# Three edits to a two-layer graph network kernel: score order in the last attention block, the last projections of layer 0, and the size of the written parts of q and k

## The chip, the cores and the metric

The kernel runs on one core of one Trainium2 chip. The metric is the device time in microseconds of one execution. PE is the matrix engine, DVE the vector engine, ACT the scalar engine, POOL the GpSimd engine and SP the sync engine, which here issues nearly all DMAs.

## The reference, cut to what matters

`x` is 3327 x 128, `adj` is a 3327 x 3327 matrix of zeros and ones. Each layer is followed by a residual and a norm.

```
# layer 0: attention by cosine over the neighbours
cos = beta * (x @ x.T) / (norm(x) @ norm(x).T + 1e-7)
x = layernorm(x + softmax(cos + (1 - adj) * -1e9) @ x)
# layer 1: attention among nodes, for d = 128 "heads" of h = 8 features
q = (x @ Wq.T).reshape(d, n, h); k = ...; v = ...
a = softmax(einsum('dnh,dmh->dnm', q, k) * d ** -0.5 + adj + adj)
out = einsum('dnm,dmh->dnh', a, v).reshape(n, h * d)
x = layernorm(x + out @ Wo.T)
```

Layer 1 has 128 score matrices of 3327 x 3327. Each needs the maximum of its rows, the exponential, and the product with v, so it is nearly the whole of the time.

## The kernel before

**Layer 0** goes over 26 tiles (T) of 128 nodes. Its loop `for t in range(-2, T + 3)` is a software pipeline: in one iteration, tile t has its scores made, tile t - 1 its weights turned and summed (`turn_weights`, `weigh0`), tile t - 2 its norm (`norm_begin`, `norm_root`, `norm_end`) and the turn of its result x1 (`project_turn`), and tile t - 3 its projection to q, k and v in six pieces of 512 columns (`project`, lines 344 to 361). All projection pieces and the turn use one PSUM bank, `pq`: a piece is a matmul, then a copy on ACT into `row`, and after two pieces a DMA of `row` to q_s, k_s or v_s in DRAM. Inside an iteration, k counts eight slots. The last two iterations of the loop hold nothing but the tail of tiles 24 and 25.

**Parting q and k** (`prepare`, lines 812 to 846) reads q_s and k_s back by heads, 16 pieces (`works`) in all. POOL reorders one into `by_t`, PE turns it 128 columns at a time, four to a chunk (`turn`), and ACT and DVE part each chunk of 512 columns in `high` (rounded to float32r) and `low` (the rest). Both are written to qp_s or kp_s, one DMA of SP each, 2 KB to a row; seven chunks make a piece, the last with 256 columns. `high` and `low` have four buffers each. Between pieces the first maxima of layer 1 are searched, and the first units are loaded.

**Layer 1** goes over 9 blocks of up to 3 tiles of queries; the last block has 2 tiles (256 queries). A block has 32 units of 4 heads each. A unit has 26 steps, one for each tile of keys. All engines take their instructions in the order in which the code writes them. A step of unit u does this:

- `shifts`: writes the negative row maxima, in three bf16 parts, in PSUM by matmuls with 3 rows; in `eb` (two heads, hs_b), later in `ea` (the two others, hs_a). Line 700.
- `scores`: adds the products of keys and queries (float32r, 32 rows a head). Line 706.
- `search`: products for the maxima of a later unit, 33 steps ahead, each reduced by DVE: a pair, `max_pair`, of two heads in the PSUM tile m2 (reduction line 619), and a single, `max_single`, in m1 (line 640). Both show as `m` on line 604. m1 and m2 have one buffer each.
- `pb`: exponential of eb on ACT (line 917), multiplied on POOL with the exponential of the adjacency (line 918).
- `add_adj`: adds twice the adjacency to ea on PE (line 687); then its exponential `pa`, one of each head (line 946).
- `weigh`: products of the step before the last with v, in `acc` (line 717).

`eb` has one buffer of two heads, `ea` one buffer for each of its two heads. When the maxima are searched for blocks of three tiles (`full`), each step has a pair and a single; the pair goes behind eb's shifts and the single behind ea's. For the last block, the single goes behind eb's shifts in each step and the pair behind ea's in every second one; this is the case for the last 33 steps of block 7 and all of block 8 but its last 33 steps, which have nothing to search. The heads of pair and single are chosen so that they use other rows of the array than the work beside them.

Of the kernel before, what the change touches and what calls it, by code (L numbers as in the profile page):

```python
# [19 lines left out]
P = 128  # L20
# [26 lines left out]
def gnn_two_layers(  # L47
# [118 lines left out]
    with ExitStack() as l0:  # L166
# [174 lines left out]
        def project_turn(t: int):  # L341
            u = tiles[t]
            tp = ps_x.tile([P, 512], F32, name="pq")
            nc.tensor.transpose(tp[:, :P], u.x1, ident)
            u.x1T = ptp.tile([P, P], F32, name="x1T")
            nc.scalar.copy(u.x1T, tp[:, :P])
# [16 lines left out]
        with tc.manual_schedule(  # L363
            engines={
                mybir.EngineType.PE,
                mybir.EngineType.Activation,
                mybir.EngineType.DVE,
                mybir.EngineType.Pool,
            }
        ):  # L370
            xn = big.tile([P, T, D], F32, name="xn")
            nc.gpsimd.memset(xn[:, T - 1, :], 0.0)
            w = (T - 1) * P
            nc.sync.dma_start(xn[:, : T - 1, :], x[:w].rearrange("(t p) d -> p t d", p=P))
            nc.sync.dma_start(xn[: N - w, T - 1, :], x[w:])
            xs = work.tile([P, T, D], F32, name="s")
            nc.gpsimd.memset(xs[:, T - 1, :], 0.0)
            xf = xs.rearrange("p t d -> p (t d)")
            for part, width in node_parts():
                nc.sync.dma_start(xf[part, :width], node_blocks(x, part, width))  # L380
            nbeta = const.tile([P, 1], F32, name="nbeta")
            nc.sync.dma_start(
                nbeta, bass.AP(tensor=beta.tensor, offset=beta.offset, ap=[[0, P], [1, 1]])
            )
            ones = const.tile([P, P], F32, name="ones")
            nc.gpsimd.memset(ones, 1.0)
            minus = const.tile([P, 1], F32, name="minus")
            nc.gpsimd.memset(minus, -1.0e9)
            for t in range(3):
                load(t)  # L390
            for t in range(2):
                load_bits(t)
            ws = []
            for name, wT in (("wq", wqT), ("wk", wkT), ("wv", wvT)):
                wt = big.tile([P, C], F32, name=name)
                nc.sync.dma_start(wt, wT)
                ws.append(wt)


            nc.gpsimd.tensor_mul(xs, xs, xs)  # L400
            norm_q = const.tile([P, T], F32, name="norm_q")
            nc.vector.reduce_sum(norm_q, xs, axis=AX.X)
            nc.scalar.activation(norm_q, norm_q, AF.Sqrt)

            nc.vector.tensor_scalar_max(norm_q, norm_q, 1e-20)
            by_q = const.tile([P, T], F32, name="by_q")
            nc.vector.reciprocal(by_q, norm_q)
            norm_c = const.tile([P, T], F32, name="norm_c")
            nc.vector.tensor_scalar_mul(norm_c, by_q, 1e-7)
            nc.vector.tensor_scalar(by_q, by_q, nbeta, -1.0, op0=ALU.mult, op1=ALU.mult)  # L410
            xT = big.tile([P, NP], F32, name="xT")
            sqT = work.tile([P, NP], F32, name="s")
            for c in range(NCH):
                tp, a, b = turn(ps_tp, lambda t: xn[:, t, :], c)
                cols = slice(a * P, b * P)
                tp = tp.rearrange("p t k -> p (t k)")
                copy(c, xT[:, cols], tp)
                nc.gpsimd.tensor_mul(sqT[:, cols], xT[:, cols], xT[:, cols])
            norm_k = big.tile([P, NP], F32, name="norm_k")
            for j in range(NPC):  # L420
                nc.scalar.activation(piece(norm_k, j), score_piece(ones, sqT, j), AF.Sqrt)
            nc.scalar.preload_act_table_set("natural_log_exp_and_others")

            for t in range(-2, T + 3):

                def there(n: int):
                    return 0 <= n < T

                for k in range(8):
                    if k == 0:  # L430
                        if there(t - 1):
                            weights(t - 1, 0)
                        if there(t - 3):
                            project(t - 3, 0)
                        if there(t - 2):
                            norm_begin(t - 2)
                        if there(t):
                            scores(t, 0)
                        if there(t - 1):
                            turn_weights(t - 1, 0)  # L440
                            weights(t - 1, 1)
                        if there(t - 3):
                            project(t - 3, 1)
                        if there(t - 2):
                            norm_root(t - 2)
                        continue
                    if there(t) and k < NPC:
                        scores(t, k)
                    if there(t - 1):
                        if k < NCH:  # L450
                            turn_weights(t - 1, k)
                        weigh0(t - 1, k - 1)
                    if k == 1 and there(t - 2):
                        norm_end(t - 2)
                    if there(t + 1):
                        for step, *i in {
                            1: ((inverse_log,),),
                            2: ((inverse_exp, 0),),
                            3: ((inverse_exp, 1), (inverse_product, 0)),
                            4: ((mask,), (inverse_newton, 0)),  # L460
                            5: ((inverse_product, 1),),
                            6: ((inverse_newton, 1),),
                        }.get(k, ()):
                            step(t + 1, *i)
                    if k < 5 and there(t - 3):
                        project(t - 3, k + 1)
                    if k == 5 and there(t - 2):
                        project_turn(t - 2)
                    if there(t + 2):
                        for i in {4: (0,), 5: (1, 2), 6: (3, 4), 7: (5, 6)}.get(k, ()):  # L470
                            adj_chunk(t + 2, i)
                    if k == 5 and there(t + 3) and t >= 0:
                        load(t + 3)
                if there(t + 4) and t + 4 > 1:
                    load_bits(t + 4)
# [8 lines left out]
    with ExitStack() as at:  # L484
# [166 lines left out]
        def search(step):  # L651
            if step is not None:
                (max_pair if len(step[1]) == 2 else max_single)(*step)
# [120 lines left out]
        with tc.manual_schedule(  # L774
# [27 lines left out]
            with ExitStack() as pr:  # L802
# [12 lines left out]
                def prepare(i):  # L815
# [9 lines left out]
                    for c in range(NCH):  # L825
                        tp, a, b = turn(ps_tp, lambda t: by_t[:, t], c)
                        tp = tp.rearrange("p t k -> p (t k)")
                        cols = slice(a * P, b * P)
                        n = (b - a) * P
                        high = work.tile([P, 512], F32R, name="high", bufs=4)[:, :n]  # L830
                        low = work.tile([P, 512], F32R, name="low", bufs=4)[:, :n]
                        nc.scalar.copy(high, tp)
                        nc.vector.tensor_sub(low, tp, high.bitcast(F32))
                        for i, part in enumerate((high, low)):
                            if b == T:

                                nc.vector.tensor_copy(
                                    part[:, n - 1 : n], part[:, n - 1 - P : n - P].bitcast(F32)
                                )
                            nc.sync.dma_start(  # L840
                                dst[g * HG : (g + 1) * HG, :, i, cols].rearrange(
                                    "d f n -> (d f) n"
                                ),
                                part.bitcast(F32),
                            )

                k = 0
                load_heads(0)
# [45 lines left out]
            for s in range(NU * T + LAG):  # L894
                i, j = divmod(s, T)
                u = us.get(i)
                if u is not None:
# [13 lines left out]
                    e_b = ps_b.tile([P, 2, 512], F32, name="eb")  # L911
                    b01 = [e_b[:, x] for x in range(2)]
                    shifts(u, b01, hs_b)
                    search(first)
                    scores(u, j, b01, hs_b, True)
                    pt_b = pp.tile([P, 2, QB], F32, name="pb")
                    nc.scalar.activation(pt_b[:, :, : u.nq], e_b[:, :, : u.nq], AF.Exp)  # L917
                    nc.gpsimd.tensor_tensor(  # L918
# [4 lines left out]
                    )  # L923
                    e_a = new_a()
                    shifts(u, e_a, hs_a)
                    search(late)
                    scores(u, j, e_a, hs_a, False)
                    free = e_a[0][:, QB:]
                    x = us.get(i + 1)
# [123 lines left out]
```

## Time and profile before

| | us |
|---|---|
| median of 3 runs | 15599.28 |
| lowest, highest | 15595.41, 15599.93 |
| the profiled execution | 15613.45 |
| its span, first to last instruction | 15611.6 |

| stage of the profiled execution | from, to (us) |
|---|---|
| layer 0 | 0 to 715 |
| parting q and k | 727 to 989 |
| layer 1, blocks of 3 tiles | 989 to 14225 |
| layer 1, last block | 14225 to 15505 |
| output projection | 15505 to 15612 |

Busy over the span: PE 98%, DVE 89%, POOL 89%, ACT 81%. Ends of matmuls are modelled, so a full PE row does not tell that the matrix array is full. In the views, x behind a group is a count of instructions, and "idle before <-releaser" names what ended an engine's wait.

### The profile page before, as it was taken

Reading aid. Unit: us, or ns where it says so; the run is one execution under the profiler, and the core shown is the slowest. Engines: PE = TensorE matmul, PEld = TensorE weight load, DVE = VectorE, ACT = ScalarE, POOL = GpSimd, SP = SyncE. Lnnn points to the kernel's source line nnn. Section 1 sums busy time; section 2 is a strip of 40 time slices with the busy share of each in tenths; the row PEclk is TensorE's granted clock in tenths of the full one; section 3 lists DMA queues with packets and bytes.
Section 4 is the critical chain, followed back from the end, with each engine's and each line's share of the span. In section 5 each row is a group of like instructions: output and inputs, shape, how many; then the busy total and the mean of one; then the engine's idle time right before and its main releaser. Section 6 shows DMA issues by size and latency. Waiting matters only on the chain.

```text
span 15611.6 us, 508271 instructions
## 1 busy us (share of the span) xinstructions
PE 15342.4 (98%) x217532; PEld 6892.6 (44%) x217532; DVE 13898.5 (89%) x16311; ACT 12601.3 (81%) x24955; POOL 13899.2 (89%) x9625
## 2 busy tenths in 40 slices
PE   8879999999999999999999999999999999999999
PEld 6634444444444444444444444444444444444555
DVE  7679999999999999999999999999999999998776
ACT  7658888888888888888888888888888888888776
POOL 0059999999999999999999999999999999999886
PEclk9879999999999999999999999999999999999999
DMA  7651111111111111111111111111111111111112
GB/s 207 204 199 47 48 51 53 50 46 50 52 51 46 50 49 54 50 46 50 53 50 46 50 53 49 50 46 56 46 50 46 50 53 50 48 48 60 60 58 75
DMA packets 631082, 973.65 MB, mean 62 GB/s; under 512 B 283568, under 2 KB 545838, under 8 KB 588368
## 3 DMA queue, kind: packets, MB, share of 16 engines
q1 hardware_dynamic: 625024, 918.99, 18.3%
q0 software_dynamic: 3792, 22.15, 0.8%
q8 instruction: 1703, 27.90, 0.8%
q14 instruction: 563, 4.61, 0.1%
HBM read 828.48 MB, written 134.61 MB: 62 GB/s over the span
## 4 chain that ended last, share of the span: by engine, by line
PE 93%; DVE 0%; issue 0%; ACT 0%; DMA 0%; POOL 0%; SPq 0%; POOLq 0%; ACTq 0%; DVEq 0%
PE acc L717 30%; PE ea L687 21%; PE m L604 16%; PE eb L700 13%; PE ea L700 10%; PE ea L706 2%; PE ea L673 1%; PE ea L735 1%; PE eb L706 1%; PE pp L1006 0%; DVE oT L147 0%; DMA qp_s<-low 0%; ACT pa L946 0%; PE tp L157 0%; DVE hid L1008 0%
## 5 line engine op out<-in xcount | busy, mean ns | idle before, releaser
L918 POOL TENSOR_TENSOR pb<-pb,eT 128x768 f32<-128x768 f32 (+1 forms) x7488 | 13190.2, 1780 | 656.3 <-ACT pb L917 374.1
L619 DVE TENSOR_REDUCE mx<-m 128x2 f32<-128x1024 f32 x6784 | 8312.5, 1225 | 970.0 <-PE eb L706 568.7
L917 ACT ACTIVATE pb<-eb 128x768 f32<-128x768 f32 (+1 forms) x7488 | 5894.9, 787 | 2497.9 <-PE eb L706 1784.2
L604 PE MATMUL m<-kx,qx 32*128 32x512 f32 (+1 forms) x23296 | 6873.5, 472 | 80.5 <-DVE mx L619 71.5
L946 ACT ACTIVATE pa<-ea 128x384 f32<-128x384 f32 (+1 forms) x14976 | 6338.4, 478 | 54.0 <-PE ea L687 14.5
L717 PE MATMUL acc<-pb,vt 128*9 128x384 f32 (+1 forms) x29952 | 5901.1, 474 | 0.1
L717 PE MATMUL acc<-pa,vt 128*9 128x384 f32 (+1 forms) x29952 | 5901.1, 474 | 0.0
L640 DVE TENSOR_REDUCE mx<-m 128x1 f32<-128x512 f32 x6400 | 4360.3, 681 | 258.5 <-PE m L604 239.9
L700 PEld LDWEIGHTS <-one 3*128 3x128 bf16 x29952 | 1469.1, 91 | 5634.9 <-issue 4656.0
L687 PE MATMUL ea<-aT,two 128*32 128x384 bf16 (+1 forms) x59904 | 3714.8, 325 | 0.0
L706 PE MATMUL eb<-qx,kx 32*128 32x384 f32 (+1 forms) x14976 | 3422.3, 453 | 0.0
L706 PE MATMUL ea<-qx,kx 32*128 32x384 f32 (+1 forms) x14976 | 3326.9, 434 | 0.0
L604 PEld LDWEIGHTS m<-kx,qx 32*128 32x128 f32 x23296 | 2825.0, 182 | 315.0 <-DVE mx L619 80.0
L700 PE MATMUL ea<-cx,one 3*128 3x384 bf16 (+1 forms) x14976 | 2744.1, 324 | 1.0
L700 PE MATMUL eb<-cx,one 3*128 3x384 bf16 (+1 forms) x14976 | 2464.3, 326 | 4.6 <-ACT pb L917 3.8
L717 PEld LDWEIGHTS acc<-pa,vt 128*9 128x9 f32 x29952 | 1412.0, 91 | 398.9
L717 PEld LDWEIGHTS acc<-pb,vt 128*9 128x9 f32 x29952 | 1411.5, 91 | 386.8 <-POOL pb L918 0.6
L687 PEld LDWEIGHTS <-two 128*32 128x32 bf16 x59904 | 945.2, 95 | 1364.4 <-issue 1171.4
L706 PEld LDWEIGHTS eb<-qx,kx 32*128 32x128 f32 x14976 | 1432.7, 188 | 0.0
L706 PEld LDWEIGHTS ea<-qx,kx 32*128 32x128 f32 x14976 | 1396.3, 182 | 7.3 <-issue 3.7
L644 DVE TENSOR_REDUCE mx<-m 128x2 f32<-128x512 f32 x1088 | 742.9, 683 | 20.6 <-PE m L604 19.3
L630 DVE TENSOR_REDUCE mx<-m 128x4 f32<-128x1024 f32 x288 | 352.8, 1225 | 46.7 <-PE m L604 28.6
(130 smaller groups left out, 4899.0 us busy)
## 6 DMA issues: line engine op xcount, KB each, us to landing
kx<-kp_s SPq DMA_DIRECT2D x576, 832.0 KB, 6.4
vn<-v_s SPq DMA_DIRECT2D x288, 416.0 KB, 3.4
qx<-qp_s SPq DMA_DIRECT2D x1024, 48.0 KB, 4.7
raw<-in_adj_dram SPq DMA_DIRECT2D x25, 1663.5 KB, 6.5
aT_s<-aT SPq DMA_DIRECT2D x26, 832.0 KB, 9.8
bits<-in_adj_dram POOLq DMA_DIRECT2D x25, 831.8 KB, 7.2
aT<-aT_s SPq DMA_DIRECT2D x208, 96.0 KB, 2.1
q_s<-row SPq DMA_DIRECT2D x26, 512.0 KB, 7.6
```

Source lines behind the costliest of these rows:

```text
L604: nc.tensor.matmul(dst, u.qx[rows(a), q * P : (q + 1) * P], u.kx[rows(a), k0:k1], start=True, stop=True,)
L619: nc.vector.tensor_reduce(u.mx[:, h, qs[0], c], m, axis=AX.X, op=ALU.max)
L630: nc.vector.tensor_reduce(dst, m.rearrange("p a (x k) -> p a x k", x=2), axis=AX.X, op=ALU.max)
L640: nc.vector.tensor_reduce(u.mx[:, a, qs[0], c : c + 1], m, axis=AX.X, op=ALU.max)
L644: nc.vector.tensor_reduce(u.mx[:, a, qs[0] : qs[1] + 1, c], m.rearrange("p (q k) -> p q k", q=2), axis=AX.X, op=ALU.max,)
L687: nc.tensor.matmul(e[r, : u.nq], two[:, r], aT[:, j, : u.nq], start=False, stop=True, tile_position=(0, 32 * c), skip_group_check=True,)
L700: nc.tensor.matmul(e[:, : u.nq], one[r], u.cx[r, : u.nq], start=True, stop=False, skip_group_check=True)
L706: nc.tensor.matmul(e[:, : u.nq], u.kx[rows(a), j * P : (j + 1) * P], u.qx[rows(a), : u.nq], start=False, stop=stop, skip_group_check=True,)
L717: nc.tensor.matmul(acc[32 * h : 32 * h + H + 1, : u.nq], u.vt[:, h, j], pts[h][:, : u.nq], start=(j == 0), stop=(j == T - 1), tile_positio ...
L917: nc.scalar.activation(pt_b[:, :, : u.nq], e_b[:, :, : u.nq], AF.Exp)
L918: nc.gpsimd.tensor_tensor(pt_b[:, :, : u.nq], pt_b[:, :, : u.nq], eT[:, j, : u.nq].unsqueeze(1).to_broadcast([P, 2, u.nq]), ALU.mult,)
L946: nc.scalar.activation(pt_a[:, h, : u.nq], e[:, : u.nq], AF.Exp)
```

## The change

Three edits:

1. In layer 1, where the maxima of the last block are searched (`full` is false), the scores of eb follow their shifts directly; the single and the pair come behind them, both ahead of ea's shifts.
2. In layer 0, tile 24 is turned in slot 1 of iteration 26, right behind its norm, and its six pieces are projected in slots 2 to 7 of that iteration, beside tile 23's; tile 25 follows in the same way in iteration 27. The loop is one iteration shorter.
3. In `prepare`, two chunks share a tile of 1024 columns of `high` and of `low`, which is written by one DMA with 4 KB to a row; the seventh chunk (256 columns) is written alone. Each has three buffers instead of four.

```
-            for t in range(-2, T + 3):
+            for t in range(-2, T + 2):
...
-                        if there(t - 3):
+                        if t <= T and there(t - 3):
                             project(t - 3, 0)
...
-                        if there(t - 3):
+                        if t <= T and there(t - 3):
                             project(t - 3, 1)
...
-                    if k < 5 and there(t - 3):
+                    if k < 5 and t <= T and there(t - 3):
                         project(t - 3, k + 1)
-                    if k == 5 and there(t - 2):
+                    if k == (5 if t < T else 1) and there(t - 2):
                         project_turn(t - 2)
+                    if t >= T and 1 < k and there(t - 2):
+                        project(t - 2, k - 2)
...
-                        cols = slice(a * P, b * P)
-                        n = (b - a) * P
-                        high = work.tile([P, 512], F32R, name="high", bufs=4)[:, :n]
-                        low = work.tile([P, 512], F32R, name="low", bufs=4)[:, :n]
+                        if c % 2 == 0:
+                            both = [
+                                work.tile([P, 2 * 512], F32R, name=name, bufs=3)
+                                for name in ("high", "low")
+                            ]
+                            start = a
+                        here = slice((a - start) * P, (b - start) * P)
+                        high, low = both[0][:, here], both[1][:, here]
                         nc.scalar.copy(high, tp)
                         nc.vector.tensor_sub(low, tp, high.bitcast(F32))
...
+                        if c % 2 or b == T:
+                            for i, part in enumerate(both):
+                                nc.sync.dma_start(
+                                    dst[
+                                        g * HG : (g + 1) * HG, :, i, start * P : b * P
+                                    ].rearrange("d f n -> (d f) n"),
+                                    part[:, :n].bitcast(F32),
+                                )
...
                     shifts(u, b01, hs_b)
-                    search(first)
+                    if full:
+                        search(first)
                     scores(u, j, b01, hs_b, True)
+                    if not full:
+                        search(first)
+                        search(late)
...
                     e_a = new_a()
                     shifts(u, e_a, hs_a)
-                    search(late)
+                    if full:
+                        search(late)
                     scores(u, j, e_a, hs_a, False)
```

More of the change, by code (lines that the diff above doesn't have):

```diff
@@ L827, in prepare @@
                         tp = tp.rearrange("p t k -> p (t k)")
-                        cols = slice(a * P, b * P)
-                        n = (b - a) * P
-                        high = work.tile([P, 512], F32R, name="high", bufs=4)[:, :n]
-                        low = work.tile([P, 512], F32R, name="low", bufs=4)[:, :n]
+                        if c % 2 == 0:
[6 more added lines that the diff above has]
+                        high, low = both[0][:, here], both[1][:, here]
                         nc.scalar.copy(high, tp)
                         nc.vector.tensor_sub(low, tp, high.bitcast(F32))
-                        for i, part in enumerate((high, low)):
-                            if b == T:
+                        n = (b - start) * P
+                        if b == T:
+                            for part in both:
                                 nc.vector.tensor_copy(
@@ L839, in prepare @@
                                 )
[L840 to L845, printed above, removed]
+                        if c % 2 or b == T:
[6 more added lines that the diff above has]
+                                )
                 k = 0
```

## The prediction

> **What bounds the kernel now.** I read the table of stretches first, because the change touches three separate stages; then each stage in the timeline. The columns are the stretch, its length, busy time (instructions) of PE, PEld, DVE, ACT and POOL, granted clock, DMA share, GB/s.
>
> ```profile
> 683.40:715.30 31.90, 23.04 (x25) 5.39 (x23) 1.96 (x9) 7.70 (x15) 0.55 (x4) 0.56 0.21 85
> 727.30:989.40 262.10, 127.83 (x554) 93.97 (x555) 137.75 (x216) 72.81 (x140) 50.41 (x24) 0.60 0.99 340
> 14224.70:15465.00 1240.30, 1239.96 (x21742) 639.25 (x21740) 974.22 (x1260) 986.10 (x2538) 1087.11 (x1019) 1.00 0.18 57
> 15465.00:15505.00 40.00, 40.00 (x689) 19.96 (x689) 0.20 (x1) 34.44 (x87) 35.38 (x30) 1.00 0.02 3
> ```
>
> The end of layer 0 (first row) is a short serial tail at half clock. Parting q and k (second row) is DMA: share 0.99. The last block of layer 1 (third row) is the large one: 31 of its 32 units of 26 steps, 40.0 us each, 1.54 us a step; its very last unit (fourth row) searches no maxima and takes 36.1 us for 26 steps.
>
> In the last block steps alternate: one has only a single search product (m1), the next has the single and a pair (m2). The timeline of PE in a pair step (start, duration):
>
> ```profile
> 14874.66 0.28 PE L700 MATMUL eb<-cx,one 3*128 3x256 bf16 x2
> 14874.67 0.50 PE L604 MATMUL m<-kx,qx 32*128 32x512 f32 x1
> 14874.70 0.36 PE L706 MATMUL eb<-qx,kx 32*128 32x256 f32 x2
> 14875.01 0.31 PE L700 MATMUL ea<-cx,one 3*128 3x256 bf16 x2
> 14875.06 0.50 PE L604 MATMUL m<-kx,qx 32*128 32x512 f32 x2
> 14875.07 0.38 PE L706 MATMUL ea<-qx,kx 32*128 32x256 f32 x2
> 14875.49 0.29 PE L687 MATMUL ea<-aT,two 128*32 128x256 bf16 x2
> ```
>
> and of ACT in it:
>
> ```profile
> 14875.30 0.60 ACT L917 ACTIVATE pb<-eb 128x512 f32<-128x512 f32 x1 [0.30 <-PE m L604]
> 14875.90 0.38 ACT L946 ACTIVATE pa<-ea 128x256 f32<-128x256 f32 x1
> ```
>
> From eb's shifts (14874.66) to the adjacency products (14875.49) is 0.83; from there to the next shifts (14876.26) 0.77, in every step. In the single step before, at 14873.22, the first part is 0.68. So 0.83 + 0.77 + 0.68 + 0.77 = 3.05 us for two steps (3.04 by the unrounded starts). The pair costs the 0.15: it starts only behind ea's shifts, which wait for the exponential of the step before (pa ends, 0.05 later the shift), and adjacency follows the pair's start by 0.43. The exponential pb is late as well: 0.64 behind its shifts, against 0.51 in the last unit (shifts 15492.07, pb 15492.58), because it is released by m, not by its own scores.
>
> The same stretch on DVE (start, duration, idle before):
>
> ```profile
> 14872.16 0.69 DVE L640 TENSOR_REDUCE mx<-m 128x1 f32<-128x512 f32 x1 [0.59 <-PE m L604]
> 14872.77 1.22 DVE L619 TENSOR_REDUCE mx<-m 128x2 f32<-128x1024 f32 x1
> 14873.90 0.68 DVE L640 TENSOR_REDUCE mx<-m 128x1 f32<-128x512 f32 x1
> 14875.20 0.69 DVE L640 TENSOR_REDUCE mx<-m 128x1 f32<-128x512 f32 x1 [0.62 <-PE m L604]
> ...
> 14899.80 0.69 DVE L640 TENSOR_REDUCE mx<-m 128x1 f32<-128x512 f32 x1 [0.59 <-PE m L604]
> ...
> 14902.81 0.69 DVE L640 TENSOR_REDUCE mx<-m 128x1 f32<-128x512 f32 x1 [0.59 <-PE m L604]
> ```
>
> Its idle time is not free room. m1 has one buffer, so single, pair, single, then the freed m1 and the next single form a ring: 0.61 (14872.16 to 14872.77) + 1.13 (to 14873.90) + 0.68 (end 14874.58) + 0.05 to PE + 0.54 (product 14874.67 to reduction 14875.20) = 3.01. Where the step is not held by PE the trace shows just that: 14899.80 and 14902.81 are 3.01 apart, as 14896.79 is from 14899.80, with the product of m waiting 0.10 behind its shifts at 14899.17. Today's 3.04 lies only 0.03 above this ring.
>
> **What the Trainium skill says.** "TensorE: Matmul & The Clock Gate", Part 3, The mechanism: matmuls on different row groups overlap, and all of them end in program order. The second half is what the trace shows: pb waits for m, which stands ahead of the scores. That starts keep program order too isn't borne out: at 14193.81 the scores of one head start before the other head's shifts (14193.83), which stand ahead of them in the program. The same page, Architectural detail: VectorE is a strict FIFO; so is the ring above. Part 1: after a slack window of about 3.4 us the clock halves; the first row's 0.56 agrees. No page prices 2 KB against 4 KB rows on this chip; I take the trace.
>
> **Part 1, the last block.** No instruction is added or removed. On PE the scores of eb go ahead of m1, and m2 goes ahead of ea's shifts. m1 and m2 read other row groups than their neighbours (m1 heads 0 or 1, m2 and eb heads 2, 3). pb is no longer held by m: 0.64 becomes 0.51. The pair no longer waits for pa: ea's shifts of the same step follow pa as they do in a single step, and adjacency comes at 0.68, not 0.83. PE alone would then need 2 x (0.68 + 0.77) = 2.90. One wait moves: m1's wait for DVE now has m2 and ea's shifts and scores queued behind it, where before it had eb's scores. As PE gets early, this wait is what ends last: the ring of 3.01. Gain 0.03 per two steps, 13 x 0.03 = 0.39 per unit. Each unit also has steps with extra work (values at j = 8, shift turns at j = 22, 23); there pairs of steps take up to 3.26, held by PE, and the earlier pair saves up to 0.1 in three of these: I take 0.16 a unit. The ring's floor per unit is 13 x 3.01 + 0.21 for the reduction of the shifts = 39.3 against 40.0, so 0.55 fits below it. 799 steps are 30.7 units: 16.9 us. Ends: 0 (all given back to the wait) and 22 (the floor). The 33 steps of the block before with the same order are near POOL's 1.85 per step at 1.89: 16 x 0.05 = 0.8 us at most, taken.
>
> **Part 2, layer 0's tail.** A piece of projection now takes 2.07 on PE and 0.69 for the copy out of the one pq bank:
>
> ```profile
> 709.86 2.07 PE L356 MATMUL pq<-wv,x1T 128*128 128x512 f32 x2 [0.69 <-ACT row L357]
> ```
>
> Twelve of these run alone after 683.2, to 715.33. Six (tile 24) move into the iteration of tile 25's weights, where PE has full clock: each 0.85 of matrix time (512 columns in two passes there), plus a wait for pq where two pieces meet: 0.85 at the turn of x1, then about 0.7 in three steps. Five of them stand ahead of the end of tile 25's sum and delay it by 5 x 0.85 + 0.85 + 3 x 0.7 = 7.2, from 683.4 to about 690.6. Then norm 1.1, root behind the last copy 1.4, rest 1.2, turn 0.7: first piece at about 695.3; six pieces of 2.77 (clock half again): 712.0. Gain 3.3 us. The six row writes move with their copies, in the same order on SP as on ACT, so nothing is overtaken; row has two buffers and a write lands in 2.6 us while a buffer is needed again after about 4. Ends: -1 to 5.
>
> **Part 3, pieces of 4 KB.** The stage is DMA, so what counts is time per byte. 979.5 to 984.5 holds only 2 KB pieces (and 113 tiny packets), 709.8 to 713 only one row write, 128 packets of 4 KB and 16 tiny ones (packets, MB, share of the 16 engines):
>
> ```profile
> q1 hardware_dynamic: 1039, 1.90, 102.3%
> ...
> q1 hardware_dynamic: 144, 0.52, 41.0%
> ```
>
> 4 KB: 0.410 x 3.2 x 16 / 128 = 164 ns. 2 KB: an engine is full over the 5 us (102.3%, so at most 5.0 x 16 / 926 = 86 ns, and 84 from the 3.5 us after 955.5). Two cost 168 to 172, one of 4 KB 164: 4 to 8 ns. 768 x 16 large packets over 16 engines: 3 to 6 us; I take 4. SP issues 96 DMAs fewer, at 0.3 to 0.6 each, but it mostly waits for ACT; nothing. Against it, each first write waits one more transpose chunk (0.85); three late pieces start with idle DMA, but the larger buffers (six chunks, not four) let ACT and DVE run ahead. Ends: -2 to 8.
>
> **Sum.** 16.9 + 0.8 + 3.3 + 4 = 25 us. The profiled execution took 15613.45 (span 15611.6); the median 15599.28 lies 14 below it; the difference carries over: 15574. 0.2%, about what a measurement of this kernel can tell from no change, is 31 us.
>
> **Rivals.** (a) The forecast: DVE's ring sets the last block: 15563 to 15588. Chance 0.70. (b) The last block gives nothing: the moved wait holds ea's shifts exactly as long as the pair did. Parts 2 and 3 alone: 15591; 0.15. For it: only 0.03 of room per two steps. (c) The ring doesn't hold: steps reach PE's 2.90, 0.145 x 400 = 58 more or less in place of 17: about 15532; 0.08. Against it: the 3.01 seen three times. (d) Slower: m1 starts only when eb's scores have streamed through, not beside them. Shifts on m1's row group follow its start by 0.34, adjacency these by 0.33. A start at 0.01 to 0.05 behind the shifts gives at most 0.72 + 0.77; the break-even with 3.04 is a start at 0.085; at 0.23 it is 2 x (0.23 + 0.34 + 0.33 + 0.77) = 3.34, +0.30 x 400 = 120 us: 15711; 0.07. Against it: other row groups' matmuls start within 0.04 of each other in the lines above.
>
> **Numbers.** Likeliest 15574. Range 15556 to 15598: holds (a) with its unknown ends and (b), leaves out (c) and (d). Faster by over 0.2%: (c), and the part of (a) with parts 2 and 3 near their upper ends, 0.28; slower 0.07; within 0.2% 0.65.
>
> **What would show it.** Right: pb 0.51 behind its shifts; single reductions of pair steps 3.01 apart; m1's product some 0.1 behind the shifts in pair steps, adjacency at 0.68 in single and about 0.8 in pair steps; last projection copy near 712. Wrong: two steps near 2.90 (c), or above 3.04 with m starting past 0.085 (d); a parting stage that isn't 3 to 6 us shorter.

## The result, and the profile after

The changed kernel takes 15572.76 us (median of 20 runs, 15566.76 to 15575.96), the kernel before, measured beside it, 15599.37 (20 runs): ratio 0.9983, 95% interval 0.9977 to 0.9988, 26.6 us. The prediction was 15574, with the greatest chance on "within 0.2%". One execution of all those below, the profiled one of the kernel "projections in two banks", ran at a granted clock of 0.45 and took 30293.57 us; that kernel's ratio leaves it out, and its profile isn't used.

The two profiled executions differ by 46.6 us of span (15611.6 and 15565.0). That is more than the medians do: the profiled execution of the kernel before was 14 us above its median, the one after (15566.76) 6 below. So the profiles show where time went, and the medians how much in all. By stage:

| stage | before | after | difference |
|---|---|---|---|
| start to tile 24's norm | 668.89 | 666.43 | -2.5, not touched |
| from there to the last projection copy | 46.44 | 42.35 | -4.1 |
| to the first `by_t` | 11.94 | 11.20 | -0.7, not touched |
| parting: first `by_t` to first `pb` | 262.1 | 250.0 | -12.1 |
| blocks 0 to 6 | 11583.0 | 11577.9 | -5.1, not touched |
| block 7 | 1652.3 | 1651.3 | -1.1 |
| last block, first to last `pb` | 1280.8 | 1259.8 | -21.0 |

The untouched rows are chance: in the profiles below, that of the one tile of three banks apart, blocks 0 to 6 lie anywhere between 11576 and 11588. Block 7 is within chance too: 1651.9 and 1652.1 in two other profiles with the old order, 1651.1 and 1652.4 in two with the new one.

The stretches of the changed kernel (stretch, length, busy time and instructions of PE, PEld, DVE, ACT and POOL, granted clock, DMA share, GB/s):

```profile
683.40:708.80 25.40, 18.47 (x47) 7.05 (x46) 2.39 (x11) 7.27 (x15) 0.59 (x4) 0.73 0.27 106
720.00:970.00 250.00, 125.96 (x554) 96.19 (x555) 135.90 (x216) 71.26 (x139) 50.45 (x24) 0.60 1.00 357
14199.20:15422.60 1223.40, 1223.36 (x21819) 687.35 (x21818) 973.40 (x1260) 1028.44 (x2548) 1091.26 (x1022) 1.00 0.19 58
```

31 units of the last block take 1223.4 us, 39.47 each. Before, they took 1244.7, 40.15 each: the stretch of 1240.3 in the prediction stops some three steps short of them. PE is "busy" all the time, as before, although it now waits more: its row cannot show the bound. The parting stage is still DMA from end to end, with 357 in place of 340 GB/s. A pair step on PE (start, duration):

```profile
14871.26 0.28 PE L702 MATMUL eb<-cx,one 3*128 3x256 bf16 x2
14871.30 0.36 PE L708 MATMUL eb<-qx,kx 32*128 32x256 f32 x2
14871.37 0.52 PE L606 MATMUL m<-kx,qx 32*128 32x512 f32 x3
14871.61 0.27 PE L702 MATMUL ea<-cx,one 3*128 3x256 bf16 x1
...
14872.04 0.40 PE L689 MATMUL ea<-aT,two 128*32 128x256 bf16 x8
...
14872.80 0.28 PE L702 MATMUL eb<-cx,one 3*128 3x256 bf16 x2
```

and `pb` on ACT in it:

```profile
14871.76 0.60 ACT L931 ACTIVATE pb<-eb 128x512 f32<-128x512 f32 x1 [0.21 <-PE eb L708]
```

`pb` is released by its own scores now, no longer by `m`, and starts 0.50 behind its shifts. m1's product stands 0.11 behind the shifts (14871.37 against 14871.26) with nothing on PE to wait for: it waits for its bank, m1. Adjacency follows at 0.78, in the single step at 0.68. DVE shows the bank:

```profile
14870.64 0.68 DVE L642 TENSOR_REDUCE mx<-m 128x1 f32<-128x512 f32 x1
14871.90 0.69 DVE L642 TENSOR_REDUCE mx<-m 128x1 f32<-128x512 f32 x1 [0.58 <-PE m L606]
14872.51 1.22 DVE L621 TENSOR_REDUCE mx<-m 128x2 f32<-128x1024 f32 x1
14873.64 0.68 DVE L642 TENSOR_REDUCE mx<-m 128x1 f32<-128x512 f32 x1
14874.90 0.69 DVE L642 TENSOR_REDUCE mx<-m 128x1 f32<-128x512 f32 x1 [0.58 <-PE m L606]
```

The single at 14870.64 frees m1 at 14871.32, and the product starts 0.05 later. Over the regular pair steps (those without extra work) of the 31 units, m1's product starts within 0.065 of such an end in 96% of the changed kernel's and in 29% of the kernel before's. The singles of pair steps are 3.00 apart, and the 0.58 of idle time is the ring's own (the loop from one product in m1 through DVE's reductions to the next): the single at 14873.64 ends at 14874.32, only then may the next product go to m1, and it is ready 0.58 later.

### The profile page after: what moved, and what is told of

Same layout as the page of the kernel before. It is cut to its first block, busy times and chain, and to the rows that moved or that the text cites. A ratio compares the mean times of both kernels' runs of the same rounds, so it can differ in the third digit from the quotient of the medians.

```text
span 15565.0 us, 507986 instructions
## 1 busy us (share of the span) xinstructions
PE 15307.9 (98%) x217532; PEld 6943.9 (45%) x217532; DVE 13890.0 (89%) x16311; ACT 12638.8 (81%) x24955; POOL 13870.0 (89%) x9625
## 4 chain that ended last, share of the span: by engine, by line
PE 93%; DVE 0%; DMA 0%; issue 0%; ACT 0%; POOL 0%; SPq 0%; POOLq 0%; DVEq 0%; ACTq 0%
PE acc L719 30%; PE ea L689 21%; PE m L606 16%; PE eb L702 13%; PE ea L702 9%; PE ea L708 2%; PE ea L675 1%; PE eb L708 1%; PE ea L737 1%; PE pp L1021 0%; DVE oT L147 0%; DMA qp_s<-low 0%; PE tp L157 0%; DVE hid L1023 0%; DVE ln_stats L134 0%
## 5 line engine op out<-in xcount | busy, mean ns | idle before, releaser
L606 PE MATMUL m<-kx,qx 32*128 32x512 f32 (+1 forms) x23296 | 6733.9, 469 | 70.3 <-DVE mx L621 62.4
L606 PEld LDWEIGHTS m<-kx,qx 32*128 32x128 f32 x23296 | 2762.8, 182 | 288.2 <-DVE mx L621 70.9
L708 PEld LDWEIGHTS ea<-qx,kx 32*128 32x128 f32 x14976 | 1429.7, 182 | 37.1 <-issue 3.3
L646 DVE TENSOR_REDUCE mx<-m 128x2 f32<-128x512 f32 x1088 | 742.2, 682 | 19.7 <-PE m L606 19.6
```

The costliest lines, as they stand in the source:

```text
L606: nc.tensor.matmul(dst, u.qx[rows(a), q * P : (q + 1) * P], u.kx[rows(a), k0:k1], start=True, stop=True,)
L646: nc.vector.tensor_reduce(u.mx[:, a, qs[0] : qs[1] + 1, c], m.rearrange("p (q k) -> p q k", q=2), axis=AX.X, op=ALU.max,)
L708: nc.tensor.matmul(e[:, : u.nq], u.kx[rows(a), j * P : (j + 1) * P], u.qx[rows(a), : u.nq], start=False, stop=stop, skip_group_check=True,)
```

## The experiments

Each kernel was measured beside the kernel before; stages are from each one's profile. "Tail" is the time from tile 24's norm to the last projection copy.

| kernel | median | before | ratio, 95% interval | last block | parting | tail |
|---|---|---|---|---|---|---|
| order of the last block alone | 15581.56 | 15601.12 | 0.9988, 0.9981 to 0.9994 | 1259.8 | 262.3 | 41.4 |
| tail alone | 15602.96 | 15601.12 | 1.0001, 0.9993 to 1.0009 | 1279.2 | 262.6 | 42.4 |
| 4 KB rows alone | 15597.07 | 15601.12 | 0.9996, 0.9988 to 1.0004 | 1279.9 | 253.0 | 46.4 |
| one tile of three banks | 25987.91 | 15601.12 | 1.6656, 1.6633 to 1.6679 | 2578.0 | 281.4 | 42.4 |
| pair late | 15584.09 | 15603.69 | 0.9987, 0.9981 to 0.9994 | 1267.1 | 250.4 | 42.9 |
| single early | 15580.85 | 15603.69 | 0.9985, 0.9978 to 0.9991 | 1263.4 | 249.8 | 42.4 |
| pair taken apart, two tiles | 15607.62 | 15603.69 | 1.0002, 0.9994 to 1.0010 | 1289.0 | 249.9 | 43.4 |
| 8 KB rows | 15561.02 | 15603.69 | 0.9972, 0.9962 to 0.9983 | 1260.4 | 233.8 | 42.3 |
| half reductions | 15553.55 | 15609.66 | 0.9964, 0.9950 to 0.9977 | 1231.7 | 250.4 | 42.4 |
| pair taken apart, three tiles | 15546.35 | 15609.66 | 0.9959, 0.9946 to 0.9971 | 1227.1 | 251.5 | 42.4 |
| projections in two banks | 15570.33 | 15609.66 | 0.9974, 0.9965 to 0.9984 | | | |
| all of the better ones | 15519.40 | 15611.05 | 0.9943, 0.9929 to 0.9956 | 1228.6 | 233.1 | 31.2 |

The median of the kernel before lies anywhere between 15599 and 15611, so ratios are compared, not times. The first three kernels are the kernel before with one edit each; all others are the changed kernel with one thing more, the last one with three.

### Each edit alone

The diffs are the three parts of the change.

> Edit 1 alone (order of scores and searches in the last block). Theory: the ring of DVE's single reductions sets the last block, and this edit carries most of the 26.6 us: pair and single step together 3.01 instead of 3.04, plus 0.16 or more in each unit's special steps; the last block some 21 us shorter (1281 to 1260 us from its first to its last pb), block 7 about 1 us, so about 15578 us, ratio 0.9986. Layer 0's tail (last projection copy near 715) and the parting stage (some 262 us from the first by_t to the first pb) as before. Rival: the gain of the whole change comes from the two small stages (18.6 us in the two profiles); then this edit gives 8 us or less, about 15591.

> Edit 2 alone (last two tiles of layer 0). Theory: only the serial tail is shorter; last projection copy near 709 instead of 715 and all after it shifted by that: 15599.4 - 6.5 = 15593, ratio 0.9996. The profile of the changed kernel says 6.5 where the prediction said 3.3. Rival: the parting stage is limited by the DMA engines, whose queue also carries the adjacency reads issued ahead of it, so that the earlier end is taken back there: last copy at 709, first pb no earlier, 15599, ratio 1.0000.

> Edit 3 alone (q and k written in rows of 4 KB). Theory by packet times: 3 to 6 us, 15595, ratio 0.9997; the parting stage some 258 us in its profile, and the profile of the kernel before (262.1) had a stage that was long by chance. Rival: larger pieces are worth the whole difference of the two profiled stages, 12 us: 15587, ratio 0.9992, stage 250 us.

The order of the last block carries most of it: 19.6 us in the medians, 1259.8 us for the block, exactly as with all three edits. The rival there is out. The tail alone shows no gain in its median, and the 4 KB rows 4 us with an interval that holds from 19 us of gain to 6 of loss, though their stage is 9 to 10 us shorter in the profile than the three of the old form (262.1, 262.3, 262.6). That is nearer to the rival's 12 than to 3 to 6. The packets of the parting stage, worked out from the trace by size, in the kernel before, the changed one and the one with 8 KB rows below (number, mean ns, their time over 16 engines):

```
            2 KB writes         4 KB writes         8 KB writes
large rows  24576 x 85.0 130.5  12288 x 160.8 123.5  4096 x 313.0  80.2
last chunks  4096 x 48.3  12.4   4096 x 47.4   12.1  4096 x 200.0  51.2
4 bytes      4496 x  8.8   2.5   2951 x  8.9    1.65 1808 x   9.1   1.0
all else               113.1               111.7               101.3
```

(The last chunks are rows of 1 KB, with 8 KB writes of 5 KB.) Two rows of 2 KB take 170, one of 4 KB 160.8: 9 ns saved, 7.0 us in all. The 4-byte packets, which come along with the DMAs, give 0.8. With the rest that is 9.5 us of DMA time. With this edit alone packet times fall by as much (9.7), but the stage by 9.1 and not 12.1; those 3 us aren't in the packets, and stay open.

Why the tail alone gains nothing shows beside the first kernel, which has the *old* order of projections and still the shortest tail, 41.4. Its pieces on PE:

```profile
691.59 1.13 PE L356 MATMUL pq<-wv,x1T 128*128 128x512 f32 x2 [0.69 <-ACT row L357]
...
694.08 1.13 PE L356 MATMUL pq<-wq,x1T 128*128 128x512 f32 x2 [0.35 <-ACT x1T L346]
695.90 1.81 PE L356 MATMUL pq<-wq,x1T 128*128 128x512 f32 x2 [0.69 <-ACT row L357]
```

Here all six pieces of tile 24 run at 1.13, full clock, and the clock falls at 696.20; in the kernel before (shown above with pieces of 2.07) it fell at 687.16. The Trainium skill has a reason that fits: "TensorE: Matmul & The Clock Gate", Part 1, What's actually happening, says that the clock is set by how busy PE was in a window of about 3.4 us that runs freely, not started by the kernel. The traces agree: periods at half clock last 3.41 us or multiples of it, and counted back from the fall in thirteen profiles, the last window has PE busy for 0.24 to 0.52 of it, while the windows ahead of it, 0.55 and more, kept the full clock. So what the prediction calls slack need not be idle: PE busy for half of a window was too little here. Loose pieces, 1.13 of PE in every 1.82, lie a little above that: the first window behind the dense work had 0.50 in the kernel before, and the clock fell; in this kernel it had 0.55, the next two 0.66, and the fall came three windows later. So the old tail took 46.4 us in two profiles and 41.4 in this one, by the phase of the windows as far as these traces tell; no run set the phase. The new order leaves PE a gap of 2.26 while tile 25's norm runs; the clock fell behind it, at 694.0 to 696.4, in all nine profiles that have it with one bank, and the tail takes 42.4, 43.4 at most. The edit saves 4 us or costs 1, and how often each is the case isn't known.

### One tile for the three banks

```
-            m = ps_m.tile([P, 2, 512], F32, name="m2")
+            m = m3[:, 0:2] if swap[0] else m3[:, 1:3]
...
-            m = ps_m.tile([P, 512], F32, name="m1")
+            m = m3[:, 2] if swap[0] else m3[:, 0]
```

> All three edits, and the searches' three PSUM banks used in turn in the last block, so that no single's product waits for the reduction just before it: single in bank 0, pair in banks 1 and 2, single in bank 0, then single in bank 2, pair in banks 0 and 1, single in bank 2, and so on. The DVE ring of 3.01 is gone, with the same instructions. Theory (the ring holds the changed kernel's last block): two steps fall from 3.01 to PE's 2.90, so 0.11 x 13 x 31 = 44 us less than with the three edits alone: about 15529 us, ratio to the kernel before 0.9955. Rival: the pair steps are held by PE or by the exponential of ea, and m's wait for DVE only fills that time: no change against the three edits, 15573, ratio 0.9983.

Neither came. The group of `m` on PE (busy, mean ns | idle before, releaser), first in this kernel, then in the changed one:

```profile
L606 PE MATMUL m<-kx,qx 32*128 32x512 f32 (+1 forms) x23296 | 7615.0, 493 | 7900.6 <-DVE mx L624 7262.9
```

```profile
L606 PE MATMUL m<-kx,qx 32*128 32x512 f32 (+1 forms) x23296 | 6733.9, 469 | 70.3 <-DVE mx L621 62.4
```

PE waits 7900 us for DVE where it waited 70: one tile is one thing to wait for, whichever of its banks is meant, and each product stands behind the reduction just before it, in the full blocks too (2790 us each in place of 1654). The edit did not build what it was to test. It took the ring's kind of wait to its extreme instead.

### Which half of the new order counts

Pair late:

```
                     if not full:
                         search(first)
-                        search(late)
...
-                    if full:
-                        search(late)
+                    search(late)
```

> All three edits, but in the last block the pair stays behind ea's shifts; only the single goes behind eb's scores. Theory: the 0.83 of the pair step (ea's shifts wait for pa, then the pair, then 0.43 to the adjacency) is back, so two steps take 3.04 to 3.05 as in the kernel before, although pb starts 0.51 behind its shifts; nearly all of the 20 us of edit 1 is gone: about 15592 us, ratio 0.9995. Rival: the gain came from the earlier pb (0.64 to 0.51), which frees PE's next shifts and POOL; then about 15573, ratio 0.9983, with pair and single step at 3.01.

Single early:

```
-                    if full:
-                        search(first)
+                    search(first)
                     scores(u, j, b01, hs_b, True)
                     if not full:
-                        search(first)
                         search(late)
```

> All three edits, but in the last block the single stays ahead of eb's scores; only the pair moves, behind eb's scores and ahead of ea's shifts. Theory: the ring makes m1's product wait some 0.11 behind eb's shifts in pair steps, and now eb's scores, and with them pb (0.64 + 0.11 = 0.75), wait with it; ACT is then with pb until 1.35 where pa could start at 1.19, and the next ea shifts come up to 0.16 late: two steps take 3.01 to 3.17, 15573 to 15640, likeliest about 15600, ratio 1.0000. Rival: pb has room, and only the pair's place counts: two steps at the ring's 3.01, 15573, ratio 0.9983.

Both keep most of the gain (12.9 and 16.6 of 20.2 us, counted from 1280.0, the mean of the three blocks with the old order). The mean time of two regular steps is 3.04 in the kernel before, 3.01 in the changed one, 3.00 with the pair late and 3.01 with the single early. With the pair late, `pb` starts at 0.50, the pair at 0.35 in place of 0.40 behind the shifts, and the adjacency at 0.78 although the pair still stands behind ea's shifts: the earlier `pb` lets `pa` end earlier, and the wait for it is gone. My theory for this kernel, that the 0.83 would come back, fell. Its 3.00 need not be the ring's: PE's own order gives 0.35 + 0.43 + 0.77 for the pair step and 1.45 for the other, 3.00 as well, and the adjacency stays at 0.78 in pair steps whether m1's product waits or not. With the single early, `pb` came at 0.73 in pair steps as expected, but little was late for it: 3.01, the rival's number. Here the ring holds: m1's product starts within 0.065 of the end of a reduction in 94% of the regular pair steps.

What both lose against the changed kernel is mostly in the steps with extra work: with the pair late, the steps at j = 9, 23 and 25 take 1.65, 1.76 and 1.54 in place of 1.53, 1.65 and 1.45.

### Is the floor the ring?

Half reductions (the ring made shorter, the instructions the same in number and order):

```
-                nc.vector.tensor_reduce(u.mx[...], m, axis=AX.X, op=ALU.max)
+                part = m if width(units[i][0]) == QB else m[:, :256]
+                nc.vector.tensor_reduce(u.mx[...], part, axis=AX.X, op=ALU.max)
```

> All three edits, but the single's reduction in the last block reads only 256 of its 512 columns (this leaves out half of the candidates for the maximum; products, orders and waits are the same). It tests the ring by its size: 0.34 + 1.13 + 0.41 + 0.05 + 0.54 = 2.47 in place of 3.00. Theory (the ring is the floor of the changed kernel): pair steps are held by PE's own order, m1 0.01 and adjacency 0.68 behind the shifts, two steps 2.90: 0.10 x 13 x 31 = 40 us off, about 15533 us, ratio to the kernel before 0.9957. Rival: a third search product in a step costs PE its 0.10 whatever DVE does (in the variant with two products in every step two steps took 3.08): two steps stay at 3.00, about 15573, ratio 0.9983.

Pair taken apart, first in two tiles, then in three:

```
# two tiles: singles in m1, the pair's heads one a step in m2's first bank
+            m = ps_m.tile([P, 512], F32, name="m1") if not other else ps_m.tile(
+                [P, 2, 512], F32, name="m2")[:, 0]
...
# three tiles: all of the last block's searches in turn
+                        ms.close()
+                        pool["m"] = ms.enter_context(
+                            tc.tile_pool(name="at_m3", bufs=3, space=PSUM, side="right"))
...
```

> All three edits, and the pair of the last block taken apart: its two heads are searched by two singles in two successive steps, in the first bank of m2, so that each step has one single in m1 and one in m2 and DVE's order alternates between the two tiles. The product of one tile runs while DVE reduces the other: the ring with its single behind single (0.68 + 0.05 + 0.54 without another tile to reduce) is gone. DVE then has 4 singles of 0.61 to 0.68 in two steps, 2.45 to 2.75. Theory (the ring holds the changed kernel at 3.01 for two steps): both steps fall to 1.45, two to 2.90, 0.11 x 13 x 31 = 44 us: about 15529 us, ratio to the kernel before 0.9955. Rival 1: pair steps are long for what they issue on PE, not for DVE: each step now has two products, no change, 15573 (0.9983). Rival 2: DVE's more numerous reductions become the bound, 4 x 0.74 = 2.96 or more: 15550 or above.

> All three edits, and in the last block the same three PSUM banks as three tiles of one bank in rotation; the pair is taken apart as in the earlier variant, one single more in each step. A product then needs the bank of the reduction three before it, not two. In the earlier variant m2's product came at 0.34, because it waited for m2's reduction of the step before, and the adjacency follows an m by 0.43. Theory: nothing waits for DVE any more, the second product comes at 0.24 and the adjacency at 0.68 in every step, both steps 1.45, two 2.90; DVE has 4 x 0.61 to 0.68 = 2.45 to 2.72 in them. About 15533 us, ratio 0.9957. Rival: DVE's reductions are still ordered behind each other and each step's second product waits as before: two steps 3.08, 15608, ratio 1.0002.

With half reductions two regular steps take 2.91, with three tiles 2.91 as well, against 3.01, and in neither do more than 1 in 100 of m's products in regular steps start within 0.065 of the end of a reduction: PE's own 2.90 is there as soon as DVE's ring is out of the way. The last block falls by 28.1 and 32.6 us. The forecast of 40 counted all 13 pairs of steps in a unit; of the five with extra work one gains with half reductions and two with three tiles. DVE with half reductions, idle 1.02 where the ring had 0.58:

```profile
14885.28 0.41 DVE L643 TENSOR_REDUCE mx<-m 128x1 f32<-128x256 f32 x1
14886.72 0.42 DVE L643 TENSOR_REDUCE mx<-m 128x1 f32<-128x256 f32 x1 [1.02 <-PE m L606]
```

The two-tile form is the instructive miss: slower by 29 us in the block than the changed kernel, with DVE busy 1.29 of 1.54 in a step. Its PE, and then the PE of the three-tile form:

```profile
14878.42 0.28 PE L704 MATMUL eb<-cx,one 3*128 3x256 bf16 x2
...
14878.77 0.50 PE L606 MATMUL m<-kx,qx 32*128 32x512 f32 x1
...
14879.19 0.40 PE L691 MATMUL ea<-aT,two 128*32 128x256 bf16 x8
```

```profile
14881.28 0.28 PE L703 MATMUL eb<-cx,one 3*128 3x256 bf16 x2
...
14881.53 0.39 PE L607 MATMUL m<-kx,qx 32*128 32x512 f32 x1
...
14881.97 0.40 PE L690 MATMUL ea<-aT,two 128*32 128x256 bf16 x8
```

In two tiles the second product comes at 0.35 behind the shifts, because m2's reduction of the step before ends at 0.30; adjacency follows it by 0.42, at 0.77. That is a new ring, through PE: product, adjacency, next step, m1's product and reduction, m2's reduction behind it, product: 0.42 + 0.77 + 0.01 + 0.54 + 0.61 + 0.68 + 0.05 = 3.08, and two steps take 3.08. With a third tile the second product comes at 0.25, and adjacency at 0.69. Same products, same reductions; only the bank that each needs was freed one reduction earlier.

### Larger rows, and the tail in two banks

```
-                        if c % 2 == 0:
+                        if c % 4 == 0:
...
-                                work.tile([P, 2 * 512], F32R, name=name, bufs=3)
+                                work.tile([P, 4 * 512], F32R, name=name, bufs=2)
...
-                        if c % 2 or b == T:
+                        if c % 4 == 3 or b == T:
```

> All three edits, with four chunks to a piece: rows of 8 KB (the last piece three chunks, 6.5 KB less 1 KB: 5 KB), two buffers of high and of low. Theory: a packet costs a fixed part and a part by the byte; from 85.0 ns at 2 KB and 160.9 at 4 KB, 9 ns and 0.0371 ns a byte, so a row of 8 KB takes 313 ns, 9 us off two of 4 KB. 768 x 8 such rows over 16 engines save 3.5 us, and the single last chunks joined to larger rows and 64 fewer DMAs some 1.5 us: the parting stage 5 us shorter than the 250 of the changed kernel, 15568, ratio 0.9980. Rival: with two buffers of four chunks the turns wait for the writes, or writes start later, and DMA idles: a stage of 250 us or more, 15573 or above.

```
-            pq = ps_x.tile([P, 512], F32, name="pq")
+            if t < T - 2:
+                pq = ps_x.tile([P, 512], F32, name="pq")
+            else:
+                pq = ps_sc.tile([P, 2, 512], F32, name="sc")[:, 0]
```

> All three edits, and the projections of tiles 24 and 25 in two PSUM tiles in turn (the scores' tiles, free by then), so that PE doesn't wait 0.69 for the copy of each piece. Theory: PE is busy nearly without a gap, five of tile 24's pieces no longer wait (2 to 3 us earlier end of tile 25's sum), and the last six pieces take 1.12 each at full clock or 2.07 at half: the last copy comes 6 us (half clock from the second piece on) to 11 us (full clock) earlier, counted from tile 24's norm (42.4 with the three edits alone). About 15565 us, ratio 0.9978. Rival: the copies into row, which has two buffers, or their writes become the bound: 3 us or less, 15570.

A row of 8 KB took 313.0 ns, the figure worked out from the two sizes before, and writes and 4-byte packets together 4.9 us less (table above). But the stage is 16 us shorter. Of the other 11, 10.4 are in the last line of the table: 2.1 MB of reads, nearly all in rows of 832 bytes and of 13 KB, as the loads of the first units have them, were no longer inside the stage, and the rest took less time a packet. Behind it DMA has room (a share of 0.16 in the blocks), so they cost nothing there. What moved them was not tested.

The two-bank tail gave ratio 0.9974 against the changed kernel's 0.9983, some 14 us, where 8 were expected; the intervals overlap. The next kernel shows the tail.

> The three edits, with the three one-bank tiles in rotation in the last block, rows of 8 KB for the parts of q and k, and the last two tiles' projections in two PSUM tiles in turn. The three touch separate stages, so the theory is that they add: last block 1227 us (32.6 less than with the three edits), parting stage 234 us (16 less), last projection copy 6 to 11 us earlier counted from tile 24's norm, in all 26.6 + 32.6 + 16 + 8 = 83 us below the kernel before: ratio 0.9947. Rival: a stage gives back what the one ahead gains (the parting stage waits for the v rows or for the adjacency reads, which are moved out of it): ratio 0.9960 or above.

They add: 91.65 us below the kernel before, ratio 0.9943. The tail takes 31.2 us in place of 42.4, the upper end of what was expected: the clock falls at 692.30 for one window only and is back at 695.71; PE was busy for all of that window. Last block 1228.6, parting 233.1.

## Why the prediction was right, and where it was not

- **The ring.** Right in the signs it named: `pb` 0.50 behind its shifts (forecast 0.51), singles of pair steps 3.00 apart (3.01), m1's product 0.11 behind the shifts (0.10), adjacency at 0.68 and 0.78 (0.68 and 0.8). Half reductions and three tiles show that the ring was the floor and that PE's 2.90 lay under it. Rival (c), 2.90 and 15532, came only with those kernels (three tiles' 0.9959 is 15535 on the result's footing). Rival (b) is out: the order alone is worth 19.6 us. Rival (d) is out: where its bank is free, in single steps, m1 starts 0.01 behind the shifts, beside eb's scores. The 0.11 of the pair step is the ring's, and costs what (d) reckoned for a late m1: 0.11 + 0.34 + 0.33 = 0.78 to the adjacency, but in one step of two.
- **The size of part 1.** Forecast 16.9 in the last block, measured 21.0 in the two profiles and 19.6 in the medians. Regular steps gave 0.035 for two (forecast 0.03). The undersized term is the steps with extra work: 0.41 a unit for those ten, against 0.16 + 5 x 0.03 = 0.31. Block 7's 0.8 isn't shown. The room below today's time was larger than it reckoned, 40.15 a unit and not 40.0. And the 36.1 us of the last unit are 25 steps from its first to its last `pb`, not 26: 1.44 each, so PE's 1.45 with one search product is hardly more than its time with none.
- **A reason that wasn't needed.** The prediction gave the fall from 0.83 to the pair, no longer behind ea's shifts. That place alone is enough (single early, 3.01), but so is the earlier `pb` alone (pair late, 3.00). The pair's place is worth some 7 us, all in the steps with extra work.
- **Part 2.** 3.3 forecast, 4.1 in the two profiles; tile 25's sum later by 8.1 (7.2), first piece 26.8 behind tile 24's norm (26.4, though the terms it adds there give 26.1). The last copy came at 708.8 (near 712), 2.5 of that from an earlier start. The step that failed is the one unstated: that the tail of before always ran at half clock from 687 on. It doesn't; by the phase of the clock's window the edit is worth 4.1 or -1.0, and alone its median shows nothing.
- **Part 3.** 4 forecast with ends -2 and 8; the stage fell by 9 to 13, one of the prediction's own signs of being wrong. The mis-sized term is the 4 KB row, 164 ns from a row write in layer 0, 160.8 in its own stage: 9 ns saved by the pair of rows and not 4 to 8. The 4-byte packets (0.8) were left out of the sum. The rest of the 12.1, 4 us, is not in the written rows: 1.4 in packets that the edit doesn't touch, the other part open.
- **The sum** was 25, measured 26.6. That it came so near is in part luck: parts 1 and 3 were too small, and yet the terms as the profiles have them, 21 + 4 + 12 = 37, exceed the medians by 10. Where the old tail takes 41.4, its 4 becomes -1, which is half of that. Where the runs without a profile spend the rest is open: the interval of the 4 KB rows alone, from 19 us of gain to 6 of loss, is too wide to tell.

## What to carry to other kernels

An engine with idle time can still set the pace, when its idle time is a part of a ring: follow one buffer from its product through the reductions queued ahead of it back to its next product, and add up. Then test it: make one part of the ring shorter, as the half reductions do, and see whether the period falls. If it does, the remedy is one more buffer in rotation, not another order. That several orders end at the same period isn't enough: with the pair late PE's own order came to the same 3.00. When one edit is worth two or three microseconds in a stretch of loose matmuls, look first at the granted clock in several executions.

## What was not expected of the hardware

- The falls of PE's clock fit a window of 3.41 us whose phase against the work differs from run to run. PE busy for 0.52 of a window lost the clock and 0.55 kept it, in one trace; layer 0's old code, unchanged, took 41.4 or 46.4 us for the tail.
- A row of 2, 4 and 8 KB written from SBUF took 85.0, 160.8 and 313.0 ns of an engine: about 9 ns for the row and 0.037 ns a byte.
- One reduction of 512 columns took 0.68, of 256 columns 0.41, of two heads 1.22: 0.14 fixed, the rest by the element. Two singles back to back took 1.29 together, 0.07 more than the pair, as the second starts 0.07 before the first ends.
